# Row sums of the second context attention: POOL adds the exponentials of two key tiles before TensorE sums them, and the reciprocal gets a fixed place

## The chip, the cores and the metric

The kernel runs on one core of one Trainium2 chip. The metric is the device time of one launch in microseconds, as the median of several runs. The core has five engines that run their own queues in order and wait for each other by semaphores: TensorE (PE in the profile, with PEld for its weight loads), VectorE (DVE), ScalarE (ACT), GpSimd (POOL) and SyncE (SP), which issues most DMAs.

## The reference

Two decoder layers on x of shape (8, 256, 512) in float32, each with an attention, an attention to a context, and a mixture of experts. The change lies in the context attention of the second layer, which takes the normalised x as queries and the context as keys and values, and works along the sequence: the 512 features are the positions, the 256 tokens are split into 8 heads of 32.

```python
def _L1_xattn_ref(q, k, v, gamma):
    N_HEAD = 8
    B, Dq, Lq = q.shape                       # 8, 256, 512
    Dv, Lk = (v.shape[-2], v.shape[-1])       # 256, 512
    ...
    qh = q.reshape(B, h, dq, Lq)              # h = 8 heads of dq = 32 tokens
    kh = k.reshape(B, h, dq, Lk)
    vh = v.reshape(B, h, dv, Lk)
    qk = jnp.einsum('bhdq,bhdl->bhql', qh, kh) * scale
    sm = jax.nn.softmax(qk, axis=-1)
    ret = jnp.einsum('bhql,bhdl->bhdq', sm, vh)
    ret = ret.reshape(B, Dv, Lq)
    return gamma * ret
...
x = x + _L1_xattn_ref(_layernorm(x, axis=-1), ctx_2048, ctx_2048, L1_xattn_gamma)
```

The softmax needs, for each head and each of 512 queries, a maximum over 512 keys, the exponentials, and their sum over 512 keys. The sum is what the change computes in another way.

## The kernel before, in words

The stage is the method `l1_cross`. A unit is one tile of 128 tokens of one batch element: NT = 16 units, each with 4 heads (32 partitions each, `head(j)`). The 512 queries and the 512 keys are both cut in HC = 4 tiles of 128. Everything is float32, and each head's matmuls use 32 rows of TensorE's array, so four heads stand side by side in it.

The loop runs over slots t, eight to a unit, from -12 (LEAD) to the end. One slot does, in this order:

- `first(g)`, with g = t + 12, so one and a half units ahead: the scores of two heads for one tile of queries, two matmuls into two of three PSUM buffers with tag `s`. The maxima over the keys (L1327, DVE) free these buffers.
- `second(t)`: the scores the other way round, keys on partitions, of the other two heads for the key tile kc = t % 8 // 2, into two of three buffers `st`; the maxima are subtracted by a second small matmul with `minus` and `mT`; ScalarE takes the exponential of each (L1276) into `e[kc]`, of which there are three buffers. Even slots do heads 2 and 3, odd ones heads 0 and 1.
- `split(u)` after a unit's last maxima (g % 8 = 7, that is in slots t % 8 = 3): DVE turns the maxima into three bf16 parts, by three casts (L1248) and two subtractions (L1251) of 128x16. `turn(u)` transposes them three slots later (`mt`, which takes an `s` buffer) and ScalarE copies them to `mT`.
- `outputs(..., "acc")` in even slots, two slots after the exponentials: values times exponentials, four matmuls of 128x512 that write the four heads' 32 rows of `acc`.
- `outputs(..., "sums")` in odd slots: sixteen matmuls of 128x128 with the constant `sel`, which add the exponentials of key tile kc over its 128 keys, into the one PSUM buffer `sums`. They accumulate over the four kc.
- `end(u)`: ScalarE copies `acc` to `o`, DVE takes the reciprocal `r` of `sums` (L1302).
- `quotient(u)`, eight slots and more later: four matmuls with the constant `spread` give each row its reciprocal (`rb`, in an `s` buffer), ScalarE copies it, POOL multiplies `o` by it (L1313) and adds the result to x (L1314).

The order of the work on TensorE is the order in which the code issues it (`mm` pins it by `keep_in_program_order`). DVE, ScalarE and POOL operations that aren't pinned are placed by the framework's scheduler, at compile time; on the chip each queue then runs strictly in that order. A buffer that is taken again waits for the last reader of its earlier content. The layer norm of a unit's queries (`begin`) runs some units ahead: DVE computes mean and variance, POOL the power -0.5 (L140, `lnr`), DVE the normalised `q` (L156). All matmuls of the helper `mm` are recorded under L100, so they are told apart by their tiles.

Of the kernel before, what the change touches and what calls it, by code (L numbers as in the profile page):

```python
# [7 lines left out]
F32 = mybir.dt.float32  # L8
# [4 lines left out]
AF = mybir.ActivationFunctionType  # L13
ALU = mybir.AluOpType
AX = mybir.AxisListType
# [3 lines left out]
P = 128  # L19
B, S, D = 8, 256, 512  # L20
T = B * S
NT = T // P
HC = D // P
LN_EPS = 1e-5
HD = 32
# [43 lines left out]
class Decoder:  # L69
# [1126 lines left out]
    def l1_cross(self):  # L1196

        nc, a = self.nc, self.a
        LEAD = 12
        with ExitStack() as ctx:
            one = ctx.enter_context(self.pool("e0c", 1))
            pool = ctx.enter_context(self.pool("e0"))
            ps = ctx.enter_context(self.psum("e0p"))
            identb = one.tile([P, P], BF16, name="identb")
            nc.vector.tensor_copy(identb, self.ident)
            minus = one.tile([P, P], BF16, name="minus")  # L1210
            nc.gpsimd.memset(minus, -1.0)
            sel, spread = self.norm["sel"], self.norm["spread"]
            vTs, unit, ending = {}, {}, {}
            head = lambda j: slice(j * HD, (j + 1) * HD)

            def begin(u):
                b, i = divmod(u, 2)
                if i == 0:
                    vTs[b] = pool.tile([P, HC, S], F32, tag="vT", name="vT", bufs=3)
                    nc.sync.dma_start(  # L1220
                        vTs[b], a["ctxT"][:, b * S : (b + 1) * S].rearrange("(c p) t -> p c t", p=P)
                    )
                k = pool.tile([P, D], F32, tag="k", name="k", bufs=4)
                nc.sync.dma_start(k, a["ctx"][b * S + i * P : b * S + (i + 1) * P, :])
                q = pool.tile([P, D], F32, tag="q", name="q", bufs=4)
                self.layernorm(pool, self.x[2 * b + i], q)
                m = pool.tile([P, HC, 4], F32, tag="m", name="m", bufs=6)
                unit[u] = dict(q=q, k=k, m=m, e={})

            def first(g):  # L1230

                w, c, h = unit[g // 8], g % 8 // 2, g % 2
                got = []
                for j in (2 * h, 2 * h + 1):
                    sc = ps.tile([P, D], F32, tag="s", name="s", bufs=3)
                    self.mm(sc, w["q"][head(j), c * P : (c + 1) * P], w["k"][head(j), :])
                    got.append((w["m"][:, c, j : j + 1], sc))
                return got

            def split(u):  # L1240


                parts = pool.tile([P, HC, P], BF16, tag="parts", name="parts")
                nc.gpsimd.memset(parts, 0.0)
                cols = parts.rearrange("p c (j s) -> p c j s", j=4)
                m = unit[u]["m"]
                for n in range(3):
                    nc.vector.tensor_copy(cols[:, :, :, n], m)  # L1248
                    if n < 2:
                        rest = pool.tile([P, HC, 4], F32, tag="m", name="m", bufs=6)  # L1250
                        nc.vector.tensor_tensor(rest, m, cols[:, :, :, n], ALU.subtract)  # L1251
                        m = rest
                unit[u]["parts"] = parts

            def turn(u):
                t = ps.tile([P, 2 * D], BF16, tag="s", name="mt", bufs=3)
                for c in range(HC):
                    self.pin(nc.tensor.transpose(t[:, c * P : (c + 1) * P], unit[u]["parts"][:, c, :], identb))
                mT = pool.tile([P, D], BF16, tag="mT", name="mT")
                nc.scalar.copy(mT, t[:, :D])  # L1260
                unit[u]["mT"] = mT

            def second(t):

                w, kc, h = unit[t // 8], t % 8 // 2, 1 - t % 2
                if h == 1:
                    w["e"][kc] = pool.tile([P, 4, D], F32, tag="e", name="e", bufs=3)
                got = []
                for j in (2 * h, 2 * h + 1):
                    st = ps.tile([P, D], F32, tag="st", name="st", bufs=3)  # L1270
                    self.mm(st, w["k"][head(j), kc * P : (kc + 1) * P], w["q"][head(j), :], stop=False)
                    got.append((j, st))
                for j, st in got:
                    at = slice(j * HD, j * HD + 3)
                    self.mm(st, minus[at, :], w["mT"][at, :], start=False)
                    nc.scalar.activation(w["e"][kc][:, j, :], st, AF.Exp, scale=SCALE)  # L1276

            def outputs(u, kc, which):
                w = unit[u]
                b, i = divmod(u, 2)  # L1280
                if kc == 0:
                    w[which] = ps.tile([P, D if which == "acc" else P], F32, tag=which, name=which)
                if which == "acc":
                    for j in range(4):
                        lhs = vTs[b][:, kc, i * P + j * HD : i * P + (j + 1) * HD]
                        self.mm(w["acc"][head(j), :], lhs, w["e"][kc][:, j, :], start=kc == 0, stop=kc == HC - 1)
                    return

                for c in range(HC):
                    for j in range(4):  # L1290
                        self.mm(
                            w["sums"][head(j), :], sel[:, 24 - 8 * c : 56 - 8 * c],
                            w["e"][kc][:, j, c * P : (c + 1) * P],
                            start=kc == 0 and c == 0, stop=kc == HC - 1 and c == HC - 1,
                        )

            def end(u):
                w = unit.pop(u)
                acc = pool.tile([P, D], F32, tag="o", name="o")
                nc.scalar.activation(acc, w["acc"], AF.Copy, scale=self.row["gamma"])  # L1300
                r = pool.tile([P, P], F32, tag="r", name="r")
                nc.vector.reciprocal(r, w["sums"])  # L1302
                ending[u] = acc, r

            def quotient(u):
                acc, r = ending.pop(u)
                t = ps.tile([P, D], F32, tag="s", name="rb", bufs=3)
                for c in range(HC):
                    blk = slice(c * P, (c + 1) * P)
                    self.mm(t[:, blk], spread[:, blk], r)  # L1310
                rb = pool.tile([P, D], F32, tag="rb", name="rb")
                nc.scalar.copy(rb, t)
                nc.gpsimd.tensor_tensor(acc, acc, rb, ALU.mult)  # L1313
                nc.gpsimd.tensor_tensor(self.x[u], self.x[u], acc, ALU.add)  # L1314

            n = 8 * NT
            for t in range(-LEAD, n + 4):
                g = t + LEAD
                if g < n:
                    if g % 8 == 0:  # L1320
                        begin(g // 8)
                    maxima = first(g)
                if 0 <= t < n:
                    second(t)
                if g < n:
                    for m, sc in maxima:
                        nc.vector.tensor_reduce(m, sc, AX.X, ALU.max)  # L1327
                    if g % 8 == 7:
                        split(g // 8)
                if g % 8 == 2 and 0 < g // 8 <= NT:  # L1330
                    turn(g // 8 - 1)


                p = t - 2
                if p >= 0:
                    u, kc = p // 8, p % 8 // 2
                    if p < n:
                        outputs(u, kc, "acc" if p % 2 == 0 else "sums")
                    if p % 8 == 7:
                        end(u)  # L1340
                    if p % 8 == 1 and u > 0:
                        quotient(u - 1)


    def l1_ffn(self):
# [277 lines left out]
```

## Time and profile before

| | before |
|---|---|
| median of 3 runs (lowest to highest) | 3473.48 us (3469.82 to 3474.89) |
| the profiled execution: its time / its span | 3475.59 us / 3473.8 us |
| mean granted clock of TensorE | 0.96 |
| the stage `l1_cross`, first s to last rb matmul | 2380.5 to 2731.8 us |
| busy share of the whole span: PE, DVE, ACT, POOL | 93%, 46%, 29%, 22% |
| maxima, L1327 (128x512 from PSUM) | 256, 686 ns each |
| exponentials, L1276 (128x512) | 256, 595 ns each |
| reciprocal, L1302 (128x128) | 16, 958 ns each |
| `sums` matmul records (128x128, 32 array columns) | 2048 |

The profile is of one execution. "Span" is from its first instruction to its last. A float32 matmul leaves two records, so 2048 records are 1024 matmuls. The granted clock is TensorE's, 1.00 being full speed. In groups of the profile a line is followed by engine, operation, tiles (out<-in), the form (partitions x elements) and the count, then the busy time, the mean duration of one in ns, and the idle time before them with what ended it.

### The profile page before, as it was taken

The page shows a single profiled execution, that of the slowest core. Times are in us where ns is not written, and L with a number is a line of the kernel's source. Part 1 is how long each engine was busy: PE and PEld are TensorE (multiplying, and loading weights), DVE is VectorE, ACT ScalarE, POOL GpSimd, SP SyncE. Part 2 cuts the span into 40 slices and gives each one's busy share as a digit, 9 for nine tenths or more (in the row PEclk, how much of TensorE's full clock was granted, in tenths as well). Part 3 has the DMA queues.
Part 4 walks back from the last instruction along what each step waited for, and adds up shares of the span by engine and source line. Part 5 has one row for each costly group of instructions (what it writes and reads, how often), then busy time and mean ns, then how long its engine had stood idle before and what let it go on. Part 6 is the DMA issues. An engine that isn't in the chain of part 4 may idle for free.

```text
span 3473.8 us, 47108 instructions
## 1 busy us (share of the span) xinstructions
PE 3244.8 (93%) x18803; PEld 2114.1 (61%) x18803; DVE 1598.9 (46%) x3784; ACT 998.7 (29%) x1959; POOL 757.5 (22%) x792
## 2 busy tenths in 40 slices
PE   6999978999999899999999668998999899999999
PEld 4666544566666687777778445563444466666665
DVE  3655579888886000000000288655666333333332
ACT  1222123333342122222222133441555322222221
POOL 2222001222234211111110276331111111111111
PEclk9999989999999999999999879997999899999999
DMA  4000010000000577777777653001000000000000
GB/s 174 2 1 1 7 64 13 15 14 13 27 15 21 178 242 232 242 235 237 237 237 230 220 143 97 1 25 55 29 26 17 34 7 6 7 6 1 7 6 13
DMA packets 106812, 272.57 MB, mean 78 GB/s; under 512 B 15136, under 2 KB 23968, under 8 KB 105696
## 3 DMA queue, kind: packets, MB, share of 16 engines
q1 hardware_dynamic: 88128, 219.16, 19.0%
q0 software_dynamic: 18464, 50.40, 5.2%
q8 instruction: 148, 2.42, 0.3%
q14 instruction: 72, 0.59, 0.1%
HBM read 235.81 MB, written 33.70 MB: 78 GB/s over the span
## 4 chain that ended last, share of the span: by engine, by line
PE 67%; DVE 12%; POOL 2%; issue 2%; DMA 2%; ACT 1%; POOLq 0%; SPq 0%; DVEq 0%; ACTq 0%
PE mm L100 18%; PE sc L100 15%; PE out L100 7%; PE w L100 6%; PE s L100 4%; PE a L100 3%; PE b L100 3%; PE sums L100 2%; PE acc L100 2%; PE st L100 2%; DVE e L509 1%; PE pt L909 1%; PE rt L100 1%; DVE acc L1049 1%; PE acc L526 1%
## 5 line engine op out<-in xcount | busy, mean ns | idle before, releaser
L100 PE MATMUL sc<-xgT,w 128*112 128x192 f32 (+1 forms) x3072 | 529.5, 328 | 0.0
L100 PEld LDWEIGHTS sc<-xgT,w 128*112 128x112 f32 (+1 forms) x3072 | 497.4, 182 | 41.1 <-issue 40.9
L935 DVE TENSOR_TENSOR aT<-act,sc 112x192 f32<-112x192 f32 (+1 forms) x192 | 68.1, 355 | 741.3 <-ACT act L934 741.3
L100 PE MATMUL mm<-xnT,w 128*128 128x256 f32 x1152 | 276.4, 396 | 21.2 <-DMA w<-in_wqkv 14.5
L100 PE MATMUL mm<-w,aT 112*128 112x512 f32 (+3 forms) x768 | 262.7, 596 | 0.0
L100 PEld LDWEIGHTS mm<-xnT,w 128*128 128x128 f32 x1152 | 224.1, 199 | 58.7 <-issue 17.3
L100 PE MATMUL w<-xnT,w 128*128 128x256 f32 x1024 | 242.8, 380 | 0.0
L100 PE MATMUL out<-w,mix 128*128 128x512 f32 x512 | 240.4, 592 | 0.0
L1466 DVE TENSOR_TENSOR h<-base,b 128x512 f32<-128x512 f32 x128 | 88.0, 688 | 326.8 <-PE b L100 326.8
L899 POOL DMA_INDIRECT xg<-xn_d,slots x96 | 91.0, 948 | 641.4 <-PE pt L909 635.1
L100 PEld LDWEIGHTS w<-xnT,w 128*128 128x128 f32 x1024 | 192.2, 190 | 61.1 <-issue 40.4
L1470 POOL TENSOR_TENSOR mix<-h 128x256 f32<-128x256 f32 x128 | 93.1, 727 | 610.3 <-DVE h L1468 548.9
L1327 DVE TENSOR_REDUCE m<-s 128x1 f32<-128x512 f32 x256 | 164.8, 686 | 101.8 <-PE s L100 83.2
L140 POOL TENSOR_TENSOR lnr<-lne,c_nhalf 128x1 f32<-128x1 f32 x112 | 65.9, 588 | 651.4 <-DVE lne L138 646.2
L100 PE MATMUL st<-q,k 32*128 32x256 f32 (+1 forms) x1024 | 196.7, 545 | 1.2 <-ACT e L505 1.2
L100 PE MATMUL mm<-mT,w 128*118 128x256 f32 (+1 forms) x768 | 175.1, 388 | 9.8 <-DVE hT L827 9.8
L1276 ACT ACTIVATE e<-st 128x512 f32<-128x512 f32 x256 | 139.0, 595 | 142.0 <-PE st L100 140.3
L934 ACT ACTIVATE act<-sc 112x192 f32<-112x192 f32 (+1 forms) x192 | 63.6, 331 | 401.9 <-PE sc L100 401.9
L100 PEld LDWEIGHTS out<-w,mix 128*128 128x128 f32 x512 | 97.3, 190 | 122.4 <-issue 119.8
L100 PEld LDWEIGHTS mm<-w,aT 112*128 112x128 f32 (+3 forms) x768 | 95.6, 163 | 122.5 <-issue 122.5
L100 PEld LDWEIGHTS mm<-mT,w 128*118 128x118 f32 (+1 forms) x768 | 141.9, 186 | 45.8 <-DVE hT L827 12.1
L100 PE MATMUL s<-k,q 32*128 32x512 f32 x512 | 160.0, 700 | 6.3 <-issue 3.5
(333 smaller groups left out, 5322.6 us busy)
## 6 DMA issues: line engine op xcount, KB each, us to landing
w<-in_Wg SPq DMA_DIRECT2D x64, 704.0 KB, 7.4
w<-in_Wu SPq DMA_DIRECT2D x64, 704.0 KB, 4.6
w<-in_Wd SPq DMA_DIRECT2D x64, 448.0 KB, 6.4
w<-in_Wd SPq DMA_DIRECT2D x64, 256.0 KB, 5.2
y_d<-yo SPq DMA_DIRECT2D x64, 256.0 KB, 3.9
y_d<-yo SPq DMA_DIRECT2D x64, 128.0 KB, 4.1
w<-in_W SPq DMA_DIRECT2D x8, 1024.0 KB, 5.3
x<-in_x SPq DMA_DIRECT2D x16, 256.0 KB, 5.5
```

The source lines that it names most:

```text
L100: self.pin(self.nc.tensor.matmul(out, lhs, rhs, start=start, stop=stop))
L140: ins = nc.gpsimd.tensor_tensor(r, e, self.nhalf[:, :n], ALU.pow)
L509: self.pin(nc.vector.scalar_tensor_tensor(e, e, 1.0, low, ALU.max, ALU.mult))
L526: self.pin(nc.tensor.matmul(acc[head(j), half(n)], lhs(j), e[:, j, :], start=kc == 0 and n == 0, stop=kc == 1, skip_group_check=True,))
L899: nc.gpsimd.indirect_dma_start(xg, None, xn_d, bass.IndirectOffsetOnAxis(ap=slots[:, i : i + 1], axis=0))
L909: self.pin(nc.tensor.transpose(t[:, blk], w[n][:, blk], self.ident))
L934: nc.scalar.activation(act[:n_m], ps[:n_m, :CAP], AF.Silu)
L935: nc.vector.tensor_tensor(w["a", h][:n_m, m, :], act[:n_m], ps[:n_m, S : S + CAP], ALU.mult)
L1276: nc.scalar.activation(w["e"][kc][:, j, :], st, AF.Exp, scale=SCALE)
L1327: nc.vector.tensor_reduce(m, sc, AX.X, ALU.max)
L1466: nc.vector.tensor_tensor(both(h), twice(base), both(t), ALU.add)
L1470: nc.gpsimd.tensor_tensor(mix, h[:, :G], h[:, G:], ALU.add)
```

## The change

- The sums of a unit are taken over two tiles of keys at once: `pair(t)` lets POOL add `e[2n]` and `e[2n+1]`, two heads (128x1024) at a time, in slots t % 4 = 2 and 3, into a new tile `two` (two buffers). `sums` then reads `two[n]`, in slots t % 4 = 3, five slots after pair began (p = t - 7). A unit has two sums steps of sixteen matmuls for four.
- The last unit isn't paired: its four sums steps read `e` as before, one slot later than its acc.
- `e` gets four buffers for three.
- The copy of `acc` to `o` is issued right behind the last acc of a unit, and no longer in `end`.
- The reciprocal (`invert`) is pinned on DVE: it is issued in slot t % 8 = 4 behind that slot's maxima, which are pinned too. `quotient` follows one slot later, t % 8 = 5 (t = 8u + 13; before, 8u + 11).
- Nothing outside `l1_cross` changes.

```diff
@@ -1225,7 +1226,7 @@
                 q = pool.tile([P, D], F32, tag="q", name="q", bufs=4)
                 self.layernorm(pool, self.x[2 * b + i], q)
                 m = pool.tile([P, HC, 4], F32, tag="m", name="m", bufs=6)
-                unit[u] = dict(q=q, k=k, m=m, e={})
+                unit[u] = dict(q=q, k=k, m=m, e={}, two={})
 
             def first(g):
 
@@ -1264,7 +1265,7 @@
 
                 w, kc, h = unit[t // 8], t % 8 // 2, 1 - t % 2
                 if h == 1:
-                    w["e"][kc] = pool.tile([P, 4, D], F32, tag="e", name="e", bufs=3)
+                    w["e"][kc] = pool.tile([P, 4, D], F32, tag="e", name="e", bufs=4)
                 got = []
                 for j in (2 * h, 2 * h + 1):
                     st = ps.tile([P, D], F32, tag="st", name="st", bufs=3)
@@ -1275,32 +1276,46 @@
                     self.mm(st, minus[at, :], w["mT"][at, :], start=False)
                     nc.scalar.activation(w["e"][kc][:, j, :], st, AF.Exp, scale=SCALE)
 
-            def outputs(u, kc, which):
+            def pair(t):
+
+                w, n, h = unit[t // 8], t % 8 // 4, 1 - t % 2
+                if h == 1:
+                    w["two"][n] = pool.tile([P, 4, D], F32, tag="two", name="two")
+                js = slice(2 * h, 2 * h + 2)
+                nc.gpsimd.tensor_tensor(
+                    w["two"][n][:, js, :], w["e"][2 * n][:, js, :], w["e"][2 * n + 1][:, js, :], ALU.add
+                )
+
+            def outputs(u, kc):
                 w = unit[u]
                 b, i = divmod(u, 2)
                 if kc == 0:
-                    w[which] = ps.tile([P, D if which == "acc" else P], F32, tag=which, name=which)
-                if which == "acc":
-                    for j in range(4):
-                        lhs = vTs[b][:, kc, i * P + j * HD : i * P + (j + 1) * HD]
-                        self.mm(w["acc"][head(j), :], lhs, w["e"][kc][:, j, :], start=kc == 0, stop=kc == HC - 1)
-                    return
-
+                    w["acc"] = ps.tile([P, D], F32, tag="acc", name="acc")
+                for j in range(4):
+                    lhs = vTs[b][:, kc, i * P + j * HD : i * P + (j + 1) * HD]
+                    self.mm(w["acc"][head(j), :], lhs, w["e"][kc][:, j, :], start=kc == 0, stop=kc == HC - 1)
+                if kc == HC - 1:
+                    w["o"] = acc = pool.tile([P, D], F32, tag="o", name="o")
+                    nc.scalar.activation(acc, w["acc"], AF.Copy, scale=self.row["gamma"])
+
+            def sums(u, e, first, last):
+
+                w = unit[u]
+                if first:
+                    w["sums"] = ps.tile([P, P], F32, tag="sums", name="sums")
                 for c in range(HC):
                     for j in range(4):
                         self.mm(
                             w["sums"][head(j), :], sel[:, 24 - 8 * c : 56 - 8 * c],
-                            w["e"][kc][:, j, c * P : (c + 1) * P],
-                            start=kc == 0 and c == 0, stop=kc == HC - 1 and c == HC - 1,
+                            e[:, j, c * P : (c + 1) * P],
+                            start=first and c == 0, stop=last and c == HC - 1,
                         )
 
-            def end(u):
+            def invert(u):
                 w = unit.pop(u)
-                acc = pool.tile([P, D], F32, tag="o", name="o")
-                nc.scalar.activation(acc, w["acc"], AF.Copy, scale=self.row["gamma"])
                 r = pool.tile([P, P], F32, tag="r", name="r")
-                nc.vector.reciprocal(r, w["sums"])
-                ending[u] = acc, r
+                self.pin(nc.vector.reciprocal(r, w["sums"]))
+                ending[u] = w["o"], r
 
             def quotient(u):
                 acc, r = ending.pop(u)
@@ -1324,22 +1339,32 @@
                     second(t)
                 if g < n:
                     for m, sc in maxima:
-                        nc.vector.tensor_reduce(m, sc, AX.X, ALU.max)
+                        self.pin(nc.vector.tensor_reduce(m, sc, AX.X, ALU.max))
                     if g % 8 == 7:
                         split(g // 8)
                 if g % 8 == 2 and 0 < g // 8 <= NT:
                     turn(g // 8 - 1)
 
 
+                if t % 4 in (2, 3) and 0 <= t < n - 8:
+                    pair(t)
                 p = t - 2
-                if p >= 0:
-                    u, kc = p // 8, p % 8 // 2
-                    if p < n:
-                        outputs(u, kc, "acc" if p % 2 == 0 else "sums")
-                    if p % 8 == 7:
-                        end(u)
-                    if p % 8 == 1 and u > 0:
-                        quotient(u - 1)
+                if 0 <= p < n and p % 2 == 0:
+                    outputs(p // 8, p % 8 // 2)
+                p = t - 7
+                if 0 <= p < n - 8 and p % 4 == 0:
+                    u, half = p // 8, p % 8 // 4
+                    sums(u, unit[u]["two"][half], half == 0, half == 1)
+                p = t - 3
+                if n - 8 <= p < n and p % 2 == 0:
+                    kc = p % 8 // 2
+                    sums(NT - 1, unit[NT - 1]["e"][kc], kc == 0, kc == HC - 1)
+
+                for behind, work in ((12, invert), (13, quotient)):
+                    if t % 8 == behind % 8 and 0 <= (t - behind) // 8 < NT - 1:
+                        work((t - behind) // 8)
+            invert(NT - 1)
+            quotient(NT - 1)
 
 
     def l1_ffn(self):
```

## The prediction

> **What bounds it now.** I read the windows view of the second context attention first, without its cold start and its drain:
>
> ```profile
> core 0: us, PE busy (x) PEld busy (x) DVE busy (x) ACT busy (x) POOL busy (x), PEclk, DMA share, GB/s
> 2425.00:2697.00 272.00, 272.00 (x3486) 115.00 (x3480) 181.18 (x340) 142.81 (x262) 45.44 (x49) 1.00 0.08 23
> ```
>
> TensorE (PE) has no gap, at the full clock (1.00); POOL is at 17%. The chain of waits stays on PE and gives the pieces of a slot (a step t of the loop):
>
> ```profile
> 2450.35 1.01 PE sums L100 x32
> 2451.36 0.63 PE s L100 x2
> ...
> 2452.00 0.41 PE s L100 x2
> 2452.41 0.23 PE st L100 x4
> 2452.65 0.99 PE acc L100 x8
> ```
>
> s, st and the correcting matmuls take 1.29 us (2451.36 to 2452.65), acc 0.99, one kc of sums 1.01. A unit is 8 x 1.29 + 4 x 0.99 + 4 x 1.01 + 1.09 (rb) + 0.33 (mt) = 19.74 us; two rb in the timeline are 19.75 apart (2499.96, 2519.71). Sixteen units are the stage, so what PE does in a unit is what the stage costs. Then the timeline, for how soon a slot's buffers come free:
>
> ```profile
> 2503.33 0.70 PE L100 MATMUL s<-k,q 32*128 32x512 f32 x2
> ...
> 2504.49 1.29 DVE L1327 TENSOR_REDUCE m<-s 128x1 f32<-128x512 f32 x2 [1.00 <-PE s L100]
> ...
> 2504.72 1.09 ACT L1276 ACTIVATE e<-st 128x512 f32<-128x512 f32 x2 [1.14 <-PE st L100]
> ```
>
> From a slot's start: maxima from 1.16 to 2.45 us, exponentials from 1.39 to 2.48. Last, what POOL's two-input additions do to VectorE (DVE): a small operation and the addition beside it, and the groups of the pieces that matter:
>
> ```profile
> 2166.38 1.25 DVE L1192 SCALAR_TENSOR_TENSOR spd<-spv,spp 128x8 f32<-128x8 f32 x1
> ```
> ```profile
> 2166.34 1.27 POOL L1132 TENSOR_TENSOR y<-y,z 128x512 f32<-128x512 f32 x1 [4.02 <-DVE spp L1191]
> ```
> ```profile
> L1192 DVE SCALAR_TENSOR_TENSOR spd<-spv,spp x8: 153/167/1254, 2031.7 to 2322.0; 128x8 f32<-128x8 f32 x8
> ```
> ```profile
> L1251 DVE TENSOR_TENSOR m<-m,parts x32: 184/185/187, 2400.1 to 2698.5; 128x16 f32<-128x16 f32 x32
> ```
> ```profile
> L1470 POOL TENSOR_TENSOR mix<-h 128x256 f32<-128x256 f32 x128 | 93.1, 727 | 610.3 <-DVE h L1468 548.9 <-PE w L100 56.7 <-PE out L100 4.7
> L1313 POOL TENSOR_TENSOR o<-o,rb 128x512 f32<-128x512 f32 x16 | 20.4, 1275 | 179.8 <-ACT rb L1312 179.8
> ```
>
> A 0.17-us DVE operation with two SBUF inputs took 1.25 us and ended at 2167.63, 0.02 after POOL's addition (2167.61). The split's subtractions (L1251, two SBUF inputs as well) never met one: 184 to 187 ns.
>
> **The change, part by part.** Slots are numbered 0 to 7 in a unit; acc stays in the even ones, sums is left in 3 and 7, rb stands in 5, mt in 6.
>
> *Removed.* Two of four sums: 2 x 1.01 = 2.02 us a unit on the bounding engine. Unit: 17.72 us.
>
> *Added, POOL.* Four additions of 128x1024. No row has that width: 727 ns for 256 columns and 1275 for 512 give 2.14 ns a column, so 2.37 us; two of the 512 rows make 2.55. I take 2.45, between. POOL's unit is then 4 x 2.45 + 1.28 + 1.27 + 0.53 + 0.55 = 13.4 us, below PE's. In its queue the pairs stand ahead of the quotient, the memset and lnr, all needed a unit or more later: 0. sums reads a pair 3 us or more after it ends: 0; if POOL fell further behind, PE would wait with everything queued on it. The fourth e buffer, and o's copy (same place in ScalarE's queue): 0.
>
> *Slot 1 is bare.* Its 1.29 us are shorter than its own consumers. With 3 st buffers, the second st of slot 2 takes the buffer of slot 1's first exponential, free at 1.39 + 0.60 + 0.05 = 2.04: 0.75 us of stall. Slot 5 is covered by rb (1.29 + 1.09). Unit: 18.47.
>
> *The split is held.* From the start of slot 2: its exponentials end at 2.48, pair 2 runs 2.55 to 5.00; slot 3 starts at 2.28, its exponentials end at 4.76, so pair 3 follows at once, 5.03 to 7.48. The maxima of slot 3 end at 4.73, and the split (3 casts, 2 subtractions, 0.23 apart) is next on DVE. By the L1192 row a subtraction gets through after 7.48, and the split ends at 8.4 and not 5.9. Queued behind it: the maxima of slot 4 (8.4 to 9.7) and the reciprocal, now pinned there (to 10.6). PE waits for both: the second s of slot 5 for the first maximum's buffer (9.1 and not 6.85), with st queued behind it; rb for the reciprocal (10.7 and not 8.15): 2.55 us. Another 0.2 comes as slot 6's second s waits for the late maxima of slot 5. Unheld, the reciprocal would end 0.1 us before rb wants it, so nothing cushions this. Ends: 0 if the split isn't held, 2.75 if it is; I take 2.75: all nine small two-input DVE operations that began under a two-input POOL operation (L1192 and L782 twice, L1181 five times) ended 0.02 to 0.03 us after it. Whether the casts are held too hardly matters (the last one comes after the subtractions anyway): 0 to 0.3. Unit: 21.2, +1.45.
>
> The Trainium skill (SBUF — State Buffer, Who interferes with whom) says that DVE and POOL share a port pair, that an instruction with two SBUF inputs or a two-port mode contends for it, and that whoever issues first keeps it for the whole instruction: this speaks against the change. By it one cast would slip in between the two pairs, and the split end 0.2 us sooner; the trace has a DVE operation (L1108, 5.93 us) held through five POOL operations in a row, so I go by that.
>
> *The clock.* At half clock the trace has only stretches of whole multiples of 3.41 us:
>
> ```profile
> 2250.58:2253.99 3.41, 1.46 (x9) 1.01 (x8) 2.86 (x7) 1.49 (x3) 2.58 (x2) 1.00 0.00 0
> 2253.99:2257.40 3.41, 3.41 (x7) 1.34 (x5) 2.45 (x7) 2.19 (x10) 0.58 (x1) 0.50 0.02 5
> 2257.40:2260.81 3.41, 3.41 (x9) 1.53 (x8) 1.63 (x5) 1.50 (x3) 1.18 (x2) 1.00 0.00 0
> ```
>
> A thin window (first row) is followed by one at half clock, a dense one by full clock. I gave each matmul record 0.83 ns a column (0.43 us for 512, the second pass on the chain; half for bf16; double at half clock), times its share of the array's rows and columns, and summed over every such window of the run: all 27 before a fall have 0.39 or less, all kept ones 0.40 or more, and the clock comes back after 0.74 or more. Held as above, PE streams only s and st (0.85 us of the array) in the 3.8 us between acc of slot 4 and rb: a window inside has 0.25. Slid over the place, it stays below 0.40 for starts from 1.65 us before that gap to 1.3 us into it: 2.95 of 3.41, so 86% of the units fall. One or two windows at half clock lose 1.4 to 3.2 us; I take 2.2, x 0.86 = 1.9. Ends 0 and 3. Unit: 23.1, +3.35.
>
> The skill's rule (TensorE: Matmul & The Clock Gate, Why this matters for your kernels) is that PE-idle gaps over about 3 us cost the clock. The longest idle here would be some 1.3 us, so by it the clock holds and the sum ends 27 us lower; the windows above decide for me.
>
> *Ends of the stage.* The first unit has bare slots 3 and 5 too, at half clock (the granted clock is 0.5 until 2421); the dense window that lifts it comes later, about 13 us: +5 (0 to 8). The last unit's first sums wait for unit 14's reciprocal (one buffer): 1.1, and bare drain slots 1.5: +3.
>
> *Sum.* 14 spacings x 3.35 = 47, + 8 = 55 us on the profiled execution's 3475.6: 3530.6. That execution is 2.1 above the median of the runs: 3529.
>
> **Rivals.** (1) The clock holds: idle pieces stay short or count otherwise. 14 x 1.45 + 6 = 26: 3500. For it: PE is never idle for a whole window; against: the 27 falls. (2) Faster: the split isn't held, since operations of 16 columns slip through between POOL's reads, as L1251's 184 to 187 ns would have it; but those never met an addition. Unit 18.47: 14 x -1.28 = -18, + 8 = -10: 3464. Decided by PE's extra wait in slot 5: below 0.7 us a unit the change gains. (3) Not held, and slot 1 hides its latency: 14 x -2.02 + 3 = -25: 3448. (4) POOL becomes the bound: only if a pair takes over 4 us (4 x 4 + 3.6 = 19.6); against: both POOL rows. That the sums aren't removed is excluded: the order of PE's instructions has 32 sums matmuls a unit for 64.
>
> **How the numbers follow.** 0.2% (7 us) is about what a measurement of this kernel tells from no change. Chances: the forecast 0.62 (3504 to 3553), rival 1 0.20, rival 2 0.13 (about half each side of 7 us), the rest 0.05. Slower 0.82, same 0.06, faster 0.12. The range 3470 to 3556 takes in the forecast's ends and rival 1, and leaves out most of rivals 2 and 3.
>
> **What would show it.** The split's subtractions at 1 to 5 us, ending with a POOL addition; rb spaced about 23 us; PE's largest wait on maxima and the reciprocal in slot 5; granted clock around 0.8 between 2440 and 2750. Wrong: subtractions at 185 ns, rb 18.5 apart; or a clock of 1.00 with rb 21 apart.

## The result, and the profile after

The changed kernel takes 3496.51 us (median of 6 runs, 3489.29 to 3499.03); the kernel before, run beside it, took 3473.18 (6 runs, 3467.54 to 3475.88). The ratio is 1.0065, 95% interval 1.0053 to 1.0077: slower by 23.3 us. The forecast was 3529 (+55); its rival 1, "the clock holds", gave 3500. The direction was right, and the size was wrong by a factor of 2.4.

The profiled execution took 3499.03 us with a span of 3497.2. The windows view of the stretch that was shown of before:

```profile
2425.00:2697.00 272.00, 263.44 (x2391) 102.05 (x2385) 198.03 (x321) 132.28 (x244) 161.48 (x98) 0.97 0.08 23
```

PE, the first busy column, was busy for all of the 272.00 us and now has 8.6 us of gaps; the granted clock is 0.97 and not 1.00. POOL went from 45 to 161 us. PE has fewer matmul records (2391 for 3486), and a unit takes longer all the same. Two rb were 19.75 us apart; now they are 21.25 apart in the first eight units, 20.4 in the later ones that have no layer norm beside them, and 22 where the clock fell.

The timeline of one unit, from slot 3 to rb in slot 5 (start, duration, engine, line, operation; in brackets the idle time before it and who ended it):

```profile
2507.47 4.82 POOL L1285 TENSOR_TENSOR two<-e 128x1024 f32<-128x1024 f32 x2 [2.73 <-ACT e L1277]
...
2508.51 1.29 DVE L1342 TENSOR_REDUCE m<-s 128x1 f32<-128x512 f32 x2 [1.92 <-PE s L100]
...
2509.90 0.20 DVE L1249 CAST parts<-m 128x16 bf16<-128x16 f32 x1
...
2510.29 2.05 DVE L1252 TENSOR_TENSOR m<-m,parts 128x16 f32<-128x16 f32 x1 [0.18 <-DVE parts L1249]
...
2510.94 1.07 PE L100 MATMUL acc<-e,vT 128*32 128x512 f32 x8
...
2512.91 1.28 DVE L1342 TENSOR_REDUCE m<-s 128x1 f32<-128x512 f32 x2
2513.65 0.69 PE L100 MATMUL s<-k,q 32*128 32x512 f32 x1 [0.59 <-DVE m L1342]
...
2514.11 0.95 DVE L1317 RECIPROCAL r<-sums 128x128 f32<-128x128 f32 x1
...
2515.11 1.16 PE L100 MATMUL rb<-r,norm 128*128 128x128 f32 x8
```

This is the held split of the prediction. Pairs 2 and 3 run on POOL from 2507.47 to 2512.29. The first cast gets in where pair 2 ends (some 2509.83), and the subtraction that starts after it takes 2.05 us and ends at 2512.34, 0.05 after pair 3. Maxima, second s, reciprocal and rb follow late, in the order foretold. The groups of the subtractions, the pairs and q's operation (minimum, median, maximum in ns):

```profile
L1252 DVE TENSOR_TENSOR m<-m,parts x32: 183/185/2267, 2402.5 to 2722.8; 128x16 f32<-128x16 f32 x32
```
```profile
L1285 POOL TENSOR_TENSOR two<-e x60: 2345/2358/2545, 2419.8 to 2730.9; 128x1024 f32<-128x1024 f32 x60
```
```profile
L156 DVE TENSOR_SCALAR q<-x,ln_mv,lnr x16: 535/1128/1443, 2382.3 to 2670.3; 128x512 f32<-128x512 f32 x16
```

A pair is 2.36 us. The median subtraction is still 185 ns, since one of the two in a unit is held and the other is free behind it; the maximum tells. The last line is one that the prediction didn't look at: q's operation (0.54 us alone) takes up to 1.44 us. Its place, in slots 0 and 1:

```profile
2498.77 2.36 POOL L1285 TENSOR_TENSOR two<-e 128x1024 f32<-128x1024 f32 x1
...
2499.97 1.43 DVE L156 TENSOR_SCALAR q<-x,ln_mv,lnr 128x512 f32<-128x512 f32 x1
...
2502.33 2.58 DVE L1342 TENSOR_REDUCE m<-s 128x1 f32<-128x512 f32 x4
...
2503.05 0.18 PEld L100 LDWEIGHTS s<-k,q 32*128 32x128 f32 x1 [0.57 <-DVE m L1342]
```

Pair 6 (to 2501.13) holds q, which ends at 2501.40; three operations of the layer norm follow, and only at 2502.33 do the maxima of slot 0 begin, beside a PE that waits for their buffers. Last, the clock, the term that mattered most. Between 2440 and 2750 us there are three stretches at half clock, each of 3.41 us (from 2451.0, 2536.3 and 2601.2), where the prediction had one or two in 86% of the units. One of them, with the window before it:

```profile
2532.87:2536.29 3.42, 2.79 (x14) 0.70 (x10) 3.32 (x8) 0.58 (x3) 0.67 (x1) 1.00 0.00 0
2536.29:2539.70 3.41, 3.35 (x16) 2.45 (x18) 1.15 (x3) 1.66 (x3) 0.57 (x1) 0.50 0.00 0
```

### The profile page after: what moved, and what is told of

It is laid out like the page before. It is cut to its first block, busy times and chain, and to the rows that moved or that the text cites. A ratio compares the mean times of both kernels' runs of the same rounds, so it can differ in the third digit from the quotient of the medians.

```text
span 3497.2 us, 45234 instructions
## 1 busy us (share of the span) xinstructions
PE 3256.1 (93%) x17843; PEld 2109.4 (60%) x17843; DVE 1630.6 (47%) x3784; ACT 997.9 (29%) x1959; POOL 895.9 (26%) x852
## 4 chain that ended last, share of the span: by engine, by line
PE 65%; DVE 15%; POOL 2%; issue 2%; DMA 2%; ACT 1%; SPq 0%; POOLq 0%; DVEq 0%; ACTq 0%
PE mm L100 18%; PE sc L100 15%; PE out L100 7%; PE w L100 6%; PE s L100 4%; PE a L100 3%; PE b L100 3%; PE st L100 2%; PE acc L100 1%; DVE e L509 1%; PE pt L909 1%; PE rt L100 1%; DVE acc L1049 1%; DVE m L1252 1%; DVE m L1342 1%
## 5 line engine op out<-in xcount | busy, mean ns | idle before, releaser
L100 PE MATMUL st<-q,k 32*128 32x256 f32 (+1 forms) x1024 | 207.3, 554 | 1.8 <-ACT e L505 1.2
L100 PE MATMUL s<-k,q 32*128 32x512 f32 x512 | 190.8, 714 | 14.1 <-DVE m L1342 7.9
```

Source lines behind the costliest of these rows:

```text
L100: self.pin(self.nc.tensor.matmul(out, lhs, rhs, start=start, stop=stop))
```

## The experiments

Theory A: POOL's additions hold small two-input VectorE work, and that makes the maxima and the reciprocal late. Rival B: the new places do it (the pinned reciprocal, the bare slot), whatever POOL does. On the clock, theory C: it falls after a window of 3.41 us in which the array is used below 0.40, the prediction's reading; rival D: it falls only when TensorE is idle for long. Ratios are to the kernel before, run beside each (medians 3470.0 to 3473.2 us). Differences between changed kernels are by medians; by the ratios they come out up to 8 us different. "Falls" are stretches below full clock between 2435 us and the last s, so without the cold start and the drain, in the one profiled execution.

| kernel | us | ratio, 95% interval | rb apart, us | falls |
|---|---|---|---|---|
| changed kernel | 3496.5 | 1.0065 (1.0053 to 1.0077) | 21.25, later 20.4 | 3 |
| no additions | 3458.1 | 0.9968 (0.9956 to 0.9979) | 18.58 | 0 |
| late split | 3468.3 | 0.9994 (0.9981 to 1.0007) | 19.37 | 0 |
| before and additions | 3533.9 | 1.0183 (1.0166 to 1.0200) | 24.2 in half of the units | 12 |
| pair 3 of 1536 | 3542.8 | 1.0216 (1.0183 to 1.0249) | 23.3 to 24.4, later from 21.5 | 11 |
| pair 3 of 1280 | 3538.0 | 1.0206 (1.0180 to 1.0232) | 23.91 | 12 |
| no pins | 3526.2 | 1.0167 (1.0151 to 1.0182) | 23 to 25 in most units | 11 |
| late split, spread | 3464.8 | 0.9981 (0.9972 to 0.9991) | 19.36, later 19.0 | 0 |
| spread | 3491.9 | 1.0065 (1.0050 to 1.0081) | 21.25, later 20.3 | 3 |
| pair 3 as 768 + 256 | 3491.7 | 1.0056 (1.0040 to 1.0071) | 21.18, later 20.3 | 2 |
| late third addition | 3468.0 | 0.9987 (0.9978 to 0.9996) | 19.62, later 18.83 | 0 |
| q moved | 3483.3 | 1.0041 (1.0025 to 1.0056) | 20.35 | 0 |
| all moved | 3460.0 | 0.9966 (0.9956 to 0.9977) | 18.72 | 0 |

**No additions.**

```diff
-                if t % 4 in (2, 3) and 0 <= t < n - 8:
-                    pair(t)
...
-                    sums(u, unit[u]["two"][half], half == 0, half == 1)
+                    sums(u, unit[u]["e"][2 * half + 1], half == 0, half == 1)
```

> The changed kernel without POOL's additions: TensorE sums the exponentials of the odd key tile of each two alone, so half of every denominator is left out; all else (32 matmuls of sums a unit, fourth e buffer, pinned maxima and reciprocal, bare slot 1) stays. Theory A (POOL's additions hold small two-input VectorE work): the two subtractions fall back from 2.05 us to 0.18, q's operation from 1.43 us to 0.54, PE's stall in slot 5 (1.9 us a unit) goes and of the 1.6 us in slots 1 and 2 only the bare slot's 0.75 stays; rb 18.5 us apart and not 21.1, so 3497 - 14 x 2.6 = 3460 us. Rival B (the pinned reciprocal and the bare slot cost it, whatever POOL does): rb stays 21 apart, 3495 us.

This form leaves the even key tiles out of the denominators; it is there for its time alone. 3458.1 us, rb 18.58 apart, with a layer norm beside the unit or without: theory A's numbers. The subtractions:

```profile
L1252 DVE TENSOR_TENSOR m<-m,parts x32: 184/185/186, 2392.9 to 2678.1; 128x16 f32<-128x16 f32 x32
```

None is held. The additions cost 38 us of time (34 by the ratios) and POOL isn't the bound; rival B keeps at most the 0.86 us by which 18.58 stands above the bare sum of 17.72.

**Late split.** The split's five operations, pinned, go behind the reciprocal; the additions stay.

```diff
                     if g % 8 == 7:
-                        split(g // 8)
...
                         work((t - behind) // 8)
+                    if behind == 12 and g % 8 == 0 and 0 < g // 8 <= NT:
+                        split(g // 8 - 1)
```

> The changed kernel with the split's five operations moved in VectorE's queue from behind the maxima of slot 3 to behind slot 4's maxima and the reciprocal, where pair 3 is over; the additions stay. Theory A: subtractions 0.18 us, the stall in slot 5 falls from 1.9 us to 0.3 or less, slots 1 and 2 stay; rb 19.4 apart in units with a layer norm, 3497 - 14 x 1.7 = 3473 us. Rival B (the reciprocal's pinned place itself is too late): rb still waits 1.5 us or more for the reciprocal, 3490 to 3500 us. If the move only shifts the hold to slot 5's maxima: 3485 us.

rb 19.37 apart, for the 19.4 expected: 1.9 us a unit are back without touching POOL, the reciprocal's place or the bare slot. But 19.4 was met by luck, as the end of slot 5 and q's place show:

```profile
2561.24 1.16 PE L100 MATMUL rb<-r,norm 128*128 128x128 f32 x8
...
2561.74 0.20 DVE L1249 CAST parts<-m 128x16 bf16<-128x16 f32 x1
2561.83 1.28 DVE L1342 TENSOR_REDUCE m<-s 128x1 f32<-128x512 f32 x2
...
2562.57 1.29 PE L100 MATMUL s<-k,q 32*128 32x512 f32 x3 [0.17 <-DVE m L1342]
...
2564.78 1.06 PE L100 MATMUL acc<-e,vT 128*32 128x512 f32 x8
...
2568.14 0.65 DVE L156 TENSOR_SCALAR q<-x,ln_mv,lnr 128x512 f32<-128x512 f32 x1
```

The subtractions are free (184 to 186 ns), but q is hardly held any more either (0.65 us), since it now begins near the end of pair 6 (2568.51); the expectation had q's loss stay. In its place stands a loss that was not expected: the split is now ahead of slot 5's maxima, slot 6's s waits for them, and from rb to the acc of slot 6 it takes 3.54 us, for 2.82 without additions. These 0.72 us are all that the units without a layer norm (19.30) have above 18.58. So the move undoes both holds and pays for the split's new place. The ten runs lie between 3464 and 3480 us; the profiled one took 3479.8 and has a stretch of 17 us at half clock in the drain (from 2709.3, after the last s at 2691.0).

**Before, with the additions alone.** The four additions and the fourth e buffer go into the kernel before; nothing reads their results.

```diff
-                    w["e"][kc] = pool.tile([P, 4, D], F32, tag="e", name="e", bufs=3)
+                    w["e"][kc] = pool.tile([P, 4, D], F32, tag="e", name="e", bufs=4)
...
+                if t % 4 in (2, 3) and 0 <= t < n - 8:
+                    pair(t)
                 p = t - 2
```

> The kernel before with POOL's additions put in at the same slots and a fourth e buffer; nothing reads their results, and the four sums a unit, the unpinned reciprocal and its place stay. Theory A: the subtractions are held about 2 us here too, the maxima of slot 4 come late, and the second s of slot 5 waits; rb 0.6 to 1.5 us further apart than 19.75: 3482 to 3494 us, I take 3487. Rival B (additions cost nothing, the loss is in the new places of sums and reciprocal): 3473 us.

A miss: 3533.9 and not 3487. Theory A holds, but the hold is longer than I had worked out. The timeline of one unit:

```profile
2538.78 4.67 POOL L1284 TENSOR_TENSOR two<-e 128x1024 f32<-128x1024 f32 x2 [3.24 <-ACT e L1276]
...
2541.24 2.25 DVE L1251 TENSOR_TENSOR m<-m,parts 128x16 f32<-128x16 f32 x1
...
2543.40 1.28 POOL L1323 TENSOR_TENSOR o<-o,rb 128x512 f32<-128x512 f32 x1
...
2543.52 1.22 DVE L1248 CAST parts<-m 128x16 bf16<-128x16 f32 x1
...
2544.75 1.26 POOL L1324 TENSOR_TENSOR x<-x,o 128x512 f32<-128x512 f32 x1
...
2544.77 1.28 DVE L1251 TENSOR_TENSOR m<-m,parts 128x16 f32<-128x16 f32 x1
...
2546.91 0.69 PE L100 MATMUL s<-k,q 32*128 32x512 f32 x1 [1.67 <-DVE m L1337]
```

In the old order rb stands in slot 3, so the quotient's two operations follow the pairs on POOL at once, and the split runs into all four: subtraction, cast and subtraction end with one POOL operation each, and get in only where one ends. PE idles 1.67 us, and the clock falls in nearly every unit (24.2 apart). The changed kernel is 37 us faster than this one (41 by the ratios); half the sums explain 14 x 2.02 = 28 of it, and the quotient's new place, away from the split, with the falls that it spares, is the likely rest. So the new places are not what costs.

**A longer pair 3, by two doses,** 1536 columns and, in a second kernel, 1280. It writes part of what pair 2 wrote again, with the same values; the columns are those of the flattened tiles.

```diff
-                js = slice(2 * h, 2 * h + 2)
+                flat = lambda tile: tile.rearrange("p j s -> p (j s)")
+                js = slice(2 * D, 4 * D) if h == 1 else slice(0, 1536 if n == 0 else 2 * D)
```

> The changed kernel with the addition of slot 3 (pair 3) 1536 columns wide in place of 1024 (it writes again half of what pair 2 wrote, same values): 1.18 us longer by 2.36 us for 1024. Held subtraction 3.2 us and not 2.05, gap from acc of slot 4 to rb 4.4 us and not 3.2. Without the clock: 14 x 1.2 = 17, so 3514 us. Theory C (the clock goes by the array's use in windows of 3.41 us, less than 0.40 drops it): this gap brings most units below 0.40, 8 or more falls between 2440 and 2750 where there were 3, about 1.9 us each: 3527 to 3540 us. Rival D (only an idle TensorE drops the clock): its longest idle is 1.8 us, falls stay at 3 or fewer, 3514 us.

> The changed kernel with the addition of slot 3 1280 columns wide in place of 1024 (256 columns of pair 2 written again): 0.59 us longer, so the gap from acc of slot 4 to rb is 3.8 us, the gap that the prediction worked with, where the changed kernel has 3.2 and the 1536-column form about 4.4. Without the clock: 14 x 0.6 = 8, 3505 us. Theory C with the prediction's own share (windows below 0.40 in 86% of the units at a gap of 3.8 us): 10 to 12 falls in the stage and about 3528 us. If the share was wrong at this gap as well: 6 falls or fewer, 3505 to 3515 us.

3542.8 and 3538.0 us, where the longer hold alone would give 3514 and 3505. Three windows of the 1280-column form, behind each other:

```profile
2478.57:2481.98 3.41, 3.41 (x56) 1.38 (x50) 3.06 (x4) 1.70 (x4) 3.33 (x2) 1.00 0.00 0
2481.98:2485.39 3.41, 2.22 (x12) 0.70 (x10) 3.31 (x7) 0.48 (x1) 1.18 (x1) 1.00 0.00 0
2485.39:2488.81 3.42, 3.42 (x17) 2.30 (x16) 1.67 (x3) 1.67 (x3) 0.00 (x0) 0.51 0.00 0
```

The thin window (PE busy 2.22 us; 0.26 of the array by the prediction's reckoning) is followed by one at half clock, and this repeats: 12 falls where there were 3. PE's longest idle time in it is 1.19 us. Theory C's number of falls for a gap of 3.8 us (10 to 12) is met; its time (some 3528 us) lies between the profiled execution, the fastest of the four with 3521.7, and the median of 3538.0. Rival D is out. PE's busy time alone doesn't explain the falls either: in the trace of before, a window with PE busy for 3.20 us (2274.46 to 2277.88) is followed by one at half clock, and one with 1.60 us (2213.02 to 2216.43) is not; by the array's share they have 0.31 and 0.45.

**No pins.** Reciprocal and maxima lose theirs; the reciprocal then stands ahead of slot 4's maxima.

```diff
-                self.pin(nc.vector.reciprocal(r, w["sums"]))
+                nc.vector.reciprocal(r, w["sums"])
...
-                        self.pin(nc.vector.tensor_reduce(m, sc, AX.X, ALU.max))
+                        nc.vector.tensor_reduce(m, sc, AX.X, ALU.max)
```

> The changed kernel with the pins of the maxima and of the reciprocal taken away, and nothing else: the reciprocal then stands in VectorE's queue right behind the split and ahead of slot 4's two maxima, for a stage long. Held split and additions stay. Theory A: rb no longer waits for the reciprocal, but slot 4's maxima end 0.95 us later and the second s of slot 5, with st behind it, waits for them: rb 0 to 0.9 us further apart than 21.1, 3497 to 3512 us, more if this brings clock falls (up to 3530). Rival B (the pinned place is what costs): rb about 1.3 us closer, 3480 us.

3526.2: the upper end of theory A's range. The timeline:

```profile
2509.05 1.12 PE L100 MATMUL s<-k,q 32*128 32x512 f32 x2
...
2510.03 0.95 DVE L1317 RECIPROCAL r<-sums 128x128 f32<-128x128 f32 x1
...
2510.90 2.53 DVE L1342 TENSOR_REDUCE m<-s 128x1 f32<-128x512 f32 x4
...
2511.58 0.69 PE L100 MATMUL s<-k,q 32*128 32x512 f32 x1 [1.42 <-DVE m L1342]
...
2512.87 1.39 PE L100 MATMUL rb<-r,norm 128*128 128x128 f32 x8
```

The reciprocal is early and makes the maxima late; acc ends at 2509.05 and rb starts 3.82 us later, where the changed kernel has 3.18 (2511.93 to 2515.11). 0.6 us more of thin work and 8 more falls; the medians are 30 us apart, the profiled executions 20 (3519.2 and 3499.0). The fixed place "behind the maxima" earns this as long as the split is held.

**Spreading the sums.** The first half's sums go half to slot 7 and half to slot 1, 8 matmuls each (16 records; the expectations from here on, and the counts below, are in records), so that no slot is bare; once on the late split, once on the changed kernel.

```diff
-                    sums(u, unit[u]["two"][half], half == 0, half == 1)
+                    sums(u, unit[u]["two"][half], half == 0, half == 1, range(2 if half == 0 else HC))
+                p = t - 9
+                if 0 <= p < n - 8 and p % 8 == 0:
+                    sums(p // 8, unit[p // 8]["two"][0], True, False, range(2, HC))
```

> The late split (19.37 us between rb), and the sums of the first two key tiles cut in halves, 16 matmuls in slot 7 and 16 in slot 1 of the next unit in place of 32 in slot 7: no slot is bare. If the bare slot's missing cover costs what the prediction says (0.75 us, of which 0.5 us of matmuls in it hide 0.5, while slot 7 loses 0.25), rb come 0.3 to 0.6 us closer: 18.9, 3468 - 7 = 3461 us. Rival (the excess over 17.72 is VectorE's layer norm and not the bare slot): 19.4, 3468 us.

> The changed kernel, split where it was, with the first sums cut in halves over slots 7 and 1: only the bare slot is undone. If it costs 0.75 us in the held kernel too: rb 0.3 to 0.6 us closer, 3490 us, with the clock falls moved by the new phase by up to 4 us either way. Rival (the hold and q decide slots 0 to 2, so that the cover changes nothing): 3497 us.

Units without a layer norm gain (19.30 to 19.01, and 20.39 to 20.27); units with one stay at 19.36 and 21.25. So while q's block stands there, it sets slots 0 to 2 and not the bare slot; the rival was right for those units. On the changed kernel the spread brings no time that can be told from none (1.0065 both). Late split and spread together are under the kernel before, 0.9981 (0.9972 to 0.9991).

**Pair 3 in two parts,** 768 columns and the 256 left, one after the other.

```diff
-                js = slice(2 * h, 2 * h + 2)
-                nc.gpsimd.tensor_tensor(
...
+                parts = [slice(2 * D, 4 * D)] if h == 1 else [slice(0, 768), slice(768, 2 * D)] if n == 0 else [slice(0, 2 * D)]
+                for js in parts:
+                    self.pin(nc.gpsimd.tensor_tensor(
```

> The changed kernel with the addition of slot 3 in two parts, 768 columns and then 256, so that VectorE can get in 0.6 us earlier between them. Theory A and C: the first subtraction ends with the 768-column part (1.5 us and not 2.05), the second may meet the rest (0.3 more): gap from acc of slot 4 to rb 2.6 to 2.9 us, no more than 2 clock falls, rb about 20.8 apart: 3480 to 3490 us. Rival (a held operation waits for all queued additions): 3497 us.

```profile
2499.65 4.96 POOL L1287 TENSOR_TENSOR two<-e 128x1024 f32<-128x1024 f32 x3 [2.73 <-ACT e L1277]
...
2502.46 1.51 DVE L1252 TENSOR_TENSOR m<-m,parts 128x16 f32<-128x16 f32 x1 [0.18 <-DVE parts L1249]
...
2504.01 0.67 DVE L1249 CAST parts<-m 128x16 bf16<-128x16 f32 x1
```

The subtraction ends with the first part, as expected; then the cast is caught by the second. The gap shrinks by 0.07 us only (3.11), rb are 0.07 closer, and 3491.7 us is a difference of 5 us that the intervals of the two ratios don't separate. My range (3480 to 3490) was too low. An operation of 16 columns is held by what runs, not by what is queued: it gets in between two additions that follow each other at once. The prediction's row L1108, of 512 columns, did not (5.93 us through five POOL operations); no run here shows what makes the difference.

**Late third addition.** The split stays; pair 3 moves behind the quotient, and the sums that read it to slot 1.

```diff
-                if t % 4 in (2, 3) and 0 <= t < n - 8:
-                    pair(t)
+                if t % 8 in (2, 6, 7) and 0 <= t < n - 8:
+                    if t % 8 == 6:
+                        pair(t - 3)
+                    pair(t)
...
-                    sums(u, unit[u]["two"][half], half == 0, half == 1)
+                    sums(u, unit[u]["two"][half], half == 0, half == 1, (2, 3) if half == 0 else range(4))
+                p = t - 9
+                if 0 <= p < n - 8 and p % 8 == 0:
+                    sums(p // 8, unit[p // 8]["two"][0], True, False, (0, 1))
```

> The split stays where it was; instead the addition of slot 3 (pair 3) is moved in POOL's queue behind the quotient's two operations, to slot 6, and the 16 sums matmuls that read it from slot 7 to slot 1 of the next unit (the 16 of pair 2 stay in slot 7), so that no slot is bare. Theory A: the split's operations begin when pair 2 ends and are not held (0.2 us, at most 0.5), slots 2 to 5 take their bare sum, q may be held by pairs 3 and 6: rb 18.2 to 18.9 us apart, 3497 - 14 x 2.6 = 3455 to 3462 us, 10 us or more below the kernel before. Rival (POOL's queue of five additions in a row reaches into the next unit's split): rb 19.5 or more, 3470 to 3490 us.

The split is free (its subtractions 184 to 188 ns), but rb are 19.62 apart and not 18.2 to 18.9. q is held in slot 0 (1.35 us), and the sums were cut by heads:

```profile
2551.00 1.07 PE L100 MATMUL sums<-two,norm 128*32 128x128 f32 x16
...
2555.57 1.08 PE L100 MATMUL sums<-two,norm 128*32 128x128 f32 x32
```

16 records of two heads take as long as 32 of four. Cut by columns instead (the late split with the sums spread), 16 records of four heads took 0.64 us:

```profile
2562.04 0.64 PE L100 MATMUL sums<-two,norm 128*32 128x128 f32 x16
```

So nothing was saved in slot 7. The units without a layer norm take 18.83: the other 0.79 comes with the layer norm's block, in which q is held.

**q moved, and all moved.** The layer norm's work gets fixed places: its statistics behind slot 7's maxima, q behind slot 5's. The second kernel adds the late third addition with whole sums (slot 1) and mt in slot 7.

```diff
                         self.pin(nc.vector.tensor_reduce(m, sc, AX.X, ALU.max))
+                    if g % 8 == 3 and g // 8 + 2 < NT:
+                        measure(g // 8 + 2)
+                    if g % 8 == 1 and g // 8 + 1 < NT:
+                        scale(g // 8 + 1)
```

`measure` holds the layer norm's statistics and `scale` q's operation, all pinned. In the second kernel also:

```diff
-                if g % 8 == 2 and 0 < g // 8 <= NT:
+                if g % 8 == 3 and 0 < g // 8 <= NT:
...
-                p = t - 7
-                if 0 <= p < n - 8 and p % 4 == 0:
-                    u, half = p // 8, p % 8 // 4
-                    sums(u, unit[u]["two"][half], half == 0, half == 1)
+                for p, half in ((t - 9, 0), (t - 11, 1)):
+                    if 0 <= p < n - 8 and p % 8 == 0:
+                        sums(p // 8, unit[p // 8]["two"][half], half == 0, half == 1)
```

> The changed kernel with the layer norm's VectorE work given fixed places: its statistics (three operations, 1.0 us) behind the maxima of slot 7, q's operation behind the maxima of slot 5, where no addition of pairs runs; in the changed kernel all four follow one another between slots 0 and 1, q held by pair 6. Held split, pins and sums stay. If this block makes the excess of slots 1 and 2 in the units with a layer norm (21.25 between rb, 20.4 in the later units without): q 0.54 us and not 1.43, units 20.4 throughout, 9 x 0.85 = 7.6 less, 3489 us, and up to 5 either way from clock falls at the new phase. Rival (slot 5 with its late maxima has no room, so that the loss only moves): 3497 us or more.

> The late third addition (pair 3 behind the quotient on POOL), with its two flaws undone: the sums of the first two key tiles whole again, all 32 in slot 1 (16 matmuls of two heads had taken as long as 32 of four), the transposes mt in slot 7 in place of slot 6, and the layer norm's work in fixed places as in the run beside it. Slot 7 is short then (1.29 + 0.4). Theory A: nothing small is held, rb 17.9 to 18.5 us apart and no clock falls: 3497 - 14 x 2.9 = 3452 to 3460 us. Rival (slot 7 as bare as slot 1 was, 0.75 us and more): 19 us, 3466 us.

In the first, q is free and the units are 20.35 throughout, as the first theory said:

```profile
L1245 DVE TENSOR_SCALAR q<-x,ln_mv,lnr x16: 534/537/546, 2369.1 to 2662.3; 128x512 f32<-128x512 f32 x16
```

With the split still held it is 13 us faster than the changed kernel by the medians, 8 by the ratios, whose intervals touch; the spacing of rb is the surer sign. The second takes 3460.0 us, 0.9966 (0.9956 to 0.9977): 11 us under the kernel before and some 35 under the changed one. Its subtractions (183 to 187 ns) and q (535 to 540) are free. Its 18.72 us are above the 17.9 to 18.5 I expected; slot 7, with mt alone, is still short (at 2562.93 us PE waits 0.22 us for maxima behind it).

## Why the prediction was right and wrong

**Removed sums and the additions' own price: right.** Without the additions a unit takes 18.58 us; the prediction's unheld unit was 18.47. A pair is 2.36 us, where the prediction took 2.45 and named 2.37 as its lower bound. POOL, at 161 of 272 us, is not the bound (rival 4).

**The held split: right as a mechanism; the unit's sum came out by two errors that cancel.** Predicted: 0.75 us for the bare slot and 2.75 for the split, 21.2 in all; measured 21.25. The bare slot was sized well: without additions a unit stands 0.86 above the bare sum of 17.72, and slots 1 and 2 there take 4.30 us (2633.36 to 2637.66) for 3.57. The held split costs 1.8 and not 2.75: the units without a layer norm take 20.39, 1.81 more than without additions, and slot 5 lost 1.89 (2511.93 to 2516.20 is 4.27, for 2.38). The other 0.86, in the units with a layer norm alone, comes from a second operation that is held and that the prediction hadn't asked for: q. Moving its block takes them away (20.35 throughout), and without additions the block costs nothing. 18.58 + 1.81 + 0.86 = 21.25; that this is also 21.2 is luck. The search for two-input operations in SBUF had left q out (one tile and two columns as inputs); the held one was found only in the trace after. Since q's share is missing in the later units, over 14 spacings the held part came to 295.0 - 276.5 = 18.5 us, less some 2.6 for the falls (0.7 to 1 each), so 16, for 14 x 1.45 = 20.

**The clock: the term that failed.** "86% of the units fall", 14 x 1.9 = 27 us; measured 3 falls and 2.6 us. The rule behind it did well: a window below 0.40 was followed by a fall here too, with a blurred edge (over all kernels, drops reach up to 0.39, and some kept windows go down to 0.32). What failed is the length of the gap between acc of slot 4 and rb that went into it: 3.8 us predicted, 3.18 measured. With the records of the changed kernel, starts of a window that stay below 0.40 cover 1.1 to 1.2 us of 3.41 in a unit: about a third, not 86%. With pair 3 at 1280 columns the gap is 3.89, these starts cover 2.9 us: 85%, the prediction's own number, and the 12 falls came. So the share was right for the gap it was given, and the gap was 0.6 us too long, made of small pieces, all on one side: pair 2 starts 0.15 us sooner and two pairs are 0.09 shorter each, so that pair 3 ends 0.26 earlier by the slot; one cast slips in between the pairs, 0.18; the maxima start 0.12 before the split's last cast has ended. The Trainium skill (SBUF — State Buffer, Who interferes with whom) has that whoever issues first keeps the port for its whole instruction; the prediction said that by this rule one cast slips in, and went against it. The cast at 2509.90 agrees with the rule: it is recorded as starting with pair 3, a few ns ahead, and took its usual 0.20 us.

The step was also fed into the sum as a fixed share, though the response is steep: 3.11, 3.18, 3.82 and 3.89 us of gap (where the clock had not fallen before it ended) gave 2, 3, 11 and 12 falls; the profiled executions took 3489.0, 3499.0, 3519.2 and 3521.7 us. A term with such an edge close by should have carried both sides with their chances; rival 1 had 0.20 and should have had about as much as the forecast.

**The skill's rule on idle gaps** (TensorE: Matmul & The Clock Gate, Why this matters for your kernels), by which the prediction's sum ended 27 us lower, came nearer for this kernel, but not by its reason: in the 1280-column form, with 1.2 us of idle time in that place in most units and 1.5 at most, the clock fell 12 times, and that form took 41 us more than the changed kernel by the medians.

**Ends.** Predicted +8, measured 23.4 - 18.5 = 4.9: 2.4 because the stage began later (2382.90 for 2380.48, not of the change), 7.5 to the first rb (67.8 for 60.2; the cold stretch lasts 47.8 us and not 41.0, as foretold by +5, 0 to 8), less 4.6 gained between the last two rb (8.87 for 13.43), which the +3 for the tail had not seen, and 0.5 behind them. Unit 15's first sums wait 1.08 us for unit 14's reciprocal, as said.

Sum of the three: 16 + 2.6 + 4.9 = 23.5, for a predicted 20 + 27 + 8 = 55.

## What to carry to other kernels

Before giving POOL two-input work in SBUF, list every small VectorE operation that could run beside it, scaled ones with column operands too, and follow who waits for each: the 0.18-us operation that becomes 2 us sits at the head of a queue. Moving either side of the meeting is enough (at a price where the new place delays something else, 0.72 us a unit in the late split), and is worth more than the work saved: in the units with a layer norm the holds cost 2.67 us (21.25 for 18.58), and the sums taken away were 2.02. The same 128x1024 additions made this kernel 23 us slower or 11 us faster by the order of the work around them. And where a clock or any other resource has a threshold, ask how far the forecast stands from it before multiplying by a share.

## What the hardware showed that I had not expected

- A unit can lock to the clock's windows. With pair 3 at 1280 columns eight of the first nine rb spacings are 23.90 to 23.93 us, which is 7.0 windows of 3.413 us: a unit that would take some 21.8 us (an estimate: 21.25 and the 0.54 us by which pair 3 is longer) falls, is stretched by some 2.1 us, and meets the next window at the same place. The opposite: with q moved, 20.35 us are 5.96 windows, the 1.1 us of bad starts move by 0.13 us a unit against the grid, and the profiled run has no fall, though each unit has its thin place. Its four runs lie between 3476 and 3486 us; that other phases make this spread is likely and not shown.
- q's operation, 128x512 from one tile and two columns, is held by a POOL addition: up to 1.44 us for 0.54.
- Sums matmuls of different heads, each into its own 32 columns of the array, take less time the more heads stand in turn: 16 records took 0.64 us in sets of four heads, and 1.07 us in sets of two, which looks as if they ran beside one another.
